# A pause in a scatter queue: a 1600-column clear against a one-element clear and a register load

## The chip, the cores and the metric
The kernel runs on one core of a Trainium2 chip. The metric is the device time of one execution in microseconds (us); the median of three runs of the kernel before is 392.05 us (391.5 to 392.49). Engines are named as the profile names them: PE is TensorE, DVE is VectorE, ACT is ScalarE, POOL is GpSimd, SP is SyncE. A "q" behind a name (POOLq, SPq) means the engine's sequencer or the transfers that it issues.

## The reference
The input is `x` of 128 x 32 x 256, that is 4096 tokens of 256 features. Two layers follow, each added to `x`.

```
# layer 0: low-rank adapters by index, then a mixture of experts
H     = x @ W.T + scaling[a] * ((x @ A[a].T) @ Bm[a].T)      # a = index of the batch row
s     = sigmoid(H @ gate_w.T)                                 # 8 experts
top 2 experts of each token; their inputs are scaled by their scores
routed = sum over k: (silu(w1 xs) * (w3 xs)) @ w2             # of the chosen expert
x     = x + routed + shared(H)
# layer 1: a conditional 32x32 mix per batch row, then Hadamard + 8-bit + ternary FFN
x     = x + FFN(mix(x))
```

What matters here is the routing of layer 0. Each token picks two of eight experts, and the kernel moves the token's row to where its expert's rows are gathered.

## The kernel before, in words
**First stage: project, route, dispatch.** The 4096 tokens are 32 tiles of 128, in 8 groups (`g`) of four. For each group, `adapt` and `project` make the rows `hc` (PE, lines 246 to 262; ACT copies them out of PSUM), and `route` finds the two experts of each token and the row that each pair gets in a DRAM buffer `xs`, which has one region per expert. The rows' numbers are in the tile `dest` (DVE, lines 271 to 334). Then `route` dispatches: for each of the group's four tiles, and for each of its two choices, one indirect transfer from POOL (line 341) scatters the tile's 128 rows of 272 columns to `xs`. That makes 64 transfers. The first group is routed in two halves, so there are nine parts (`p`).

After every second tile, that is after every four transfers, and in all groups but the last two, POOL executes a pause (line 354): a memset of a tile `pause`, which nothing reads. There are 12. The code keeps a pause in program order, and `tc.issue_after(paused[-1].ins)` queues the transfers that follow behind the last pause. Outside of that, a scheduler places the instructions of each engine. POOL's first-stage queue is: some memsets, four transfers, pause, four transfers, pause, and so on, with one gather for the second layer (`wc`, line 463) after the fourth pause, and 16 transfers without a pause at the end.

Meanwhile PE goes on to the shared expert (`shared`, lines 128 to 172) of six of the eight groups, and DVE makes the ternary weights (lines 358 to 394) and a table of tiles of rows (`slot_table`). `pad` writes zeros behind each region, from SP.

**Second stage: the experts.** `fetch` (line 528, SP) reads tiles of 128 rows of `xs` into `xin`. As the rows that it reads can come from any transfer of the dispatch, it waits for all 64. Then `turn_rows` transposes them (line 536), `gate_up` and `down` multiply by the expert's weights (lines 562 and 588), and POOL scatters the results to `yt` (line 595; these transfers have a bound `NY - 1` given as a constant). This runs in 36 steps of two tiles each, and the remaining two groups of the shared expert follow it.

**Third stage.** `combine` reads `yt` back, and the second layer runs in 16 steps of two tiles (lines 640 to 797).

Of the kernel before, what the change touches and what calls it, by code (L numbers as in the profile page):

```python
# [7 lines left out]
F32 = mybir.dt.float32  # L8
F16 = mybir.dt.float16
BF16 = mybir.dt.bfloat16  # L10
I32 = mybir.dt.int32
# [4 lines left out]
P = 128  # L16
# [6 lines left out]
E = 8  # L23
# [7 lines left out]
REG = 2 * B * T  # L31
# [20 lines left out]
def tile_kernel(  # L52
# [15 lines left out]
    nc = tc.nc  # L68
# [5 lines left out]
    small = ctx.enter_context(tc.tile_pool(name="small", bufs=3))  # L74
# [3 lines left out]
    def bank(tag, name, shape=(P, 512), dtype=F32):  # L78
        return psum.tile(list(shape), dtype, tag=tag, name=name)
# [33 lines left out]
    with tc.tile_pool(name="moe", bufs=1) as moe, tc.tile_pool(name="work1", bufs=2) as work1:  # L113
# [61 lines left out]
        with tc.tile_pool(name="stage", bufs=1) as stage:  # L175
# [28 lines left out]
            nc.sync.dma_start(ud, updown)  # L204

            zeros = stage.tile([P, ROW], F32, name="zeros")
            pause = stage.tile([P, 1600], F32, name="pause")
            cnt = stage.tile([P, E], F32, name="cnt")
            nc.gpsimd.memset(zeros, 0.0)
            nc.gpsimd.memset(cum[:, 0], 0.0)  # L210
# [53 lines left out]
            def route(p, g, tiles):  # L264

                n0, m = tiles.start, len(tiles)
                part = slice(n0, n0 + m)
                lg = hc[g][:, part, D:PROW]
                s = small.tile([P, m, E], F32, tag="s", name=f"s{p}")

                nc.vector.tensor_scalar(s, lg, -88.0, None, ALU.max)
                nc.scalar.activation(s, s, AF.Exp, scale=-1.0)
                nc.vector.tensor_scalar(s, s, 1.0, None, ALU.add)
                nc.vector.reciprocal(s, s)

                sj = s.unsqueeze(2).to_broadcast([P, m, E, E])
                se = s.unsqueeze(3).to_broadcast([P, m, E, E])
                gt = small.tile([P, m, E, E], F32, tag="gt", name=f"gt{p}")
                eq = small.tile([P, m, E, E], F32, tag="eq", name=f"eq{p}")
                nc.vector.tensor_tensor(gt, sj, se, ALU.is_gt)  # L280
                nc.vector.tensor_tensor(eq, sj, se, ALU.is_equal)
                eqf = eq.rearrange("p n e j -> p n (e j)")
                nc.vector.tensor_tensor(
                    eqf,
                    eqf,
                    tri.rearrange("p e j -> p (e j)").unsqueeze(1).to_broadcast([P, m, E * E]),
                    ALU.mult,
                )
                nc.vector.tensor_tensor(gt, gt, eq, ALU.add)
                rank = small.tile([P, m, E], F32, tag="rank", name=f"rank{p}")  # L290
                nc.vector.tensor_reduce(rank, gt, AX.X, ALU.add)
                chosen = small.tile([P, m, E], BF16, tag="ch", name=f"chosen{p}")
                nc.vector.tensor_scalar(chosen, rank, 2.0, None, ALU.is_lt)  # L293

                nc.vector.scalar_tensor_tensor(lg, rank, 2.0, s, ALU.is_lt, ALU.mult)

                to = small.tile([P, m, E], F32, tag="to", name=f"to{p}")
                t2 = pj[:, C_T2 + g * GT + n0 : C_T2 + g * GT + n0 + m]
                nc.vector.tensor_tensor(
                    to, rank, t2.unsqueeze(2).to_broadcast([P, m, E]), ALU.add  # L300
                )
                nc.vector.scalar_tensor_tensor(
                    hc[g][:, part, PROW:], rank, 2.0, to, ALU.is_lt, ALU.mult
                )


                before = small.tile([P, m, E], BF16, tag="before", name=f"before{p}")
                nc.vector.tensor_copy(before[:, 0], cum[:, p])  # L308
                for n in range(1, m):
                    nc.vector.tensor_tensor(  # L310
                        before[:, n], before[:, n - 1], chosen[:, n - 1], ALU.add
                    )
                nc.vector.tensor_tensor(
                    cum[:, p + 1], before[:, m - 1], chosen[:, m - 1], ALU.add
                )
                pp = bank("x", f"pp{p}", (P, m, E))
                nc.tensor.matmul(pp, upper, chosen, start=True, stop=False)
                nc.tensor.matmul(pp, onb, before, start=False, stop=True)
                row = small.tile([P, m, E], F32, tag="row", name=f"row{p}")
                nc.vector.tensor_tensor(  # L320
                    row,
                    pp,
                    pj[:, C_EREG : C_EREG + E].unsqueeze(1).to_broadcast([P, m, E]),
                    ALU.add,
                )
                pick = small.tile([P, 2, m, E], F32, tag="pick", name=f"pick{p}")
                for i in range(2):
                    nc.vector.scalar_tensor_tensor(
                        pick[:, i], rank, float(i), row, ALU.is_equal, ALU.mult
                    )  # L330
                df = small.tile([P, 2, m], F32, tag="df", name=f"df{p}")
                dest = small.tile([P, 2, m], I32, tag="dest", name=f"dest{p}", bufs=NG + 1)
                nc.vector.tensor_reduce(df, pick, AX.X, ALU.add)
                nc.vector.tensor_copy(dest, df)

                for n in range(m):
                    with ExitStack() as stack:
                        if paused:
                            stack.enter_context(tc.issue_after(paused[-1].ins))
                        for i in range(2):  # L340
                            ins = nc.gpsimd.indirect_dma_start(  # L341
                                out=xs,
                                out_offset=bass.IndirectOffsetOnAxis(
                                    ap=dest[:, i, n : n + 1], axis=0
                                ),
                                in_=hc[g][:, n0 + n],
                                in_offset=None,
                            ).ins
                            tc.declare_no_dep(ins, group="xs", reason="every pair has its own row")
                            tc.add_to_no_dep_group("xs", ins)  # L350
                    if n % 2 and g < NG - 2:


                        paused.append(tc.keep_in_program_order(nc.gpsimd.memset(pause, 0.0)))

            paused = []

            def ternary_weights():
                rs = stage.tile([P, 2], F32, name="rs")
# [121 lines left out]
            for g in range(1, NG):  # L481
                xa = adapt(g)
                if g == 1:
                    route(0, *parts[0])
                for n in range(GT):
                    if n == GT - 1:
                        route(g, *parts[g])
                    project(g, n, xa)
                if g == 2:
                    mixes()  # L490
            for g in range(NG):
                xg.append(cpool.tile([P, GT, D], F32, tag="x", name=f"x{g}", bufs=NG))
                nc.sync.dma_start(xg[g], xt[g])
            route(NG, *parts[NG])
            tc.keep_in_program_order(nc.vector.tensor_copy(idh, ident))
            slot_table()
# [424 lines left out]
```

## Time and profile before

| what | us |
|---|---|
| median of three runs | 392.05 |
| the profiled execution, its own time | 394.07 |
| its span, first to last instruction | 392.3 |
| PE busy | 349.2 (89%) |
| DVE busy | 248.4 (63%) |
| POOL busy | 244.0 (62%) |
| POOL, 64 dispatch transfers, line 341 | 63.5 |
| POOL, 12 pauses, line 354 | 17.4 |

The profiled execution ran 2.0 us longer than the median, and 1.8 us of its time lie outside of its span. [...] Idle time of an engine is put down to what released it; "issue" is time in which the profile shows no other wait.

### The profile page before, as it was taken

The page shows a single profiled execution, that of the slowest core. Times are in us where ns is not written, and L with a number is a line of the kernel's source. Part 1 is how long each engine was busy: PE and PEld are TensorE (multiplying, and loading weights), DVE is VectorE, ACT ScalarE, POOL GpSimd, SP SyncE. Part 2 cuts the span into 40 slices and gives each one's busy share as a digit, 9 for nine tenths or more (in the row PEclk, how much of TensorE's full clock was granted, in tenths as well). Part 3 has the DMA queues.
Part 4 walks back from the last instruction along what each step waited for, and adds up shares of the span by engine and source line. Part 5 has one row for each costly group of instructions (what it writes and reads, how often), then busy time and mean ns, then how long its engine had stood idle before and what let it go on. Part 6 is the DMA issues. An engine that isn't in the chain of part 4 may idle for free.

```text
span 392.3 us, 6604 instructions
## 1 busy us (share of the span) xinstructions
PE 349.2 (89%) x2057; PEld 275.6 (70%) x2057; DVE 248.4 (63%) x764; ACT 161.1 (41%) x329; POOL 244.0 (62%) x271
## 2 busy tenths in 40 slices
PE   4998999779990799999999999997799999999873
PEld 3675666546560588888787888855689898899762
DVE  1367986999740456465555555435778878877742
ACT  1112222222110144444344344331668787778742
POOL 4058888888874035555555365548899797855520
PEclk9999999999997599999999999999999999999986
DMA  7996458543233725555444442226523352101111
GB/s 267 420 410 232 150 181 249 181 160 128 91 115 105 222 88 156 167 158 157 148 155 149 141 136 74 83 63 232 179 94 107 103 168 82 48 34 57 53 55 53
DMA packets 37906, 57.38 MB, mean 146 GB/s; under 512 B 8941, under 2 KB 27631, under 8 KB 37488
## 3 DMA queue, kind: packets, MB, share of 16 engines
q1 hardware_dynamic: 30912, 39.06, 31.0%
q0 software_dynamic: 6672, 17.84, 12.4%
q8 instruction: 17, 0.28, 0.3%
q14 instruction: 17, 0.14, 0.1%
q10 hardware_dynamic: 288, 0.07, 0.1%
HBM read 33.81 MB, written 24.18 MB: 148 GB/s over the span
## 4 chain that ended last, share of the span: by engine, by line
PE 54%; DVE 17%; issue 9%; POOL 7%; DMA 6%; ACT 5%; SPq 1%; DVEq 0%; POOLq 0%; ACTq 0%
PE pg L562 14%; PE pr L752 7%; PE po L588 6%; PE ph L260 4%; POOL yt L595 3%; PE pf L668 3%; PE py L648 3%; PE pt_s L536 3%; DMA xs<-hc,dest 2%; PE ph L261 2%; PE pu L722 2%; PE pa L246 2%; DMA xT<-in_xT 2%; DVE chosen L293 2%; PE phd L579 1%
## 5 line engine op out<-in xcount | busy, mean ns | idle before, releaser
L595 POOL DMA_INDIRECT yt<-y,to x72 | 70.0, 973 | 68.1 <-DVE cm L545 23.7
L341 POOL DMA_INDIRECT xs<-hc,dest x64 | 63.5, 992 | 36.3 <-DVE before L308 18.6
L562 PE MATMUL pg<-wall,xTs 128*128 x288 | 78.7, 399 | 2.8 <-DVE cm L545 2.0
L562 PEld LDWEIGHTS pg<-wall,xTs 128*128 128x128 f32 x288 | 50.8, 195 | 14.8 <-DVE hid L571 4.6
L571 DVE SCALAR_TENSOR_TENSOR hid<-pg,c,sil 128x128 f32<-128x128 f32 x72 | 25.1, 348 | 44.3 <-ACT sil L570 42.5
L570 ACT ACTIVATE sil<-pg,c 128x128 f32<-128x128 f32 x72 | 26.4, 367 | 60.2 <-PE pg L562 60.0
L640 POOL TENSOR_TENSOR x<-x,y 128x512 f32<-128x512 f32 x32 | 40.5, 1268 | 6.3 <-DMA y<-yt 5.0
L588 PE MATMUL po<-wall,hidT 128*128 x144 | 37.7, 381 | 0.0
L752 PE MATMUL pr<-cst,b 128*128 128x128 f32 x256 | 35.8, 288 | 1.0 <-POOL b L741 0.5
L262 ACT COPY hc<-ph 128x264 f32<-128x264 f32 x32 | 12.1, 378 | 57.2 <-PE ph L261 51.4
L260 PE MATMUL ph<-pj,xT 128*128 128x264 f32 x128 | 35.2, 399 | 0.0
L536 PE MATMUL pt_s<-cst,xin 128*128 128x128 f32 x144 | 26.2, 286 | 9.1 <-DMA xin<-xs 9.1
L752 PEld LDWEIGHTS pr<-cst,b 128*128 128x128 f32 x256 | 32.0, 198 | 1.6 <-POOL b L741 0.9
L260 PEld LDWEIGHTS ph<-pj,xT 128*128 128x128 f32 x128 | 24.3, 194 | 8.1 <-issue 3.5
L143 PE MATMUL pgs<-hT,ws 128*128 128x512 f32 x64 | 29.1, 596 | 0.8 <-DVE hT L86 0.8
L536 PEld LDWEIGHTS pt_s<-cst,xin 128*128 128x128 f32 x144 | 19.1, 147 | 14.5 <-DMA xin<-xs 10.5
L588 PEld LDWEIGHTS po<-wall,hidT 128*128 128x128 f32 x144 | 24.5, 190 | 2.2 <-ACT hidT L88 0.3
L766 ACT ACTIVATE q<-pr,half,sc 128x512 f16<-128x512 f32 x32 | 23.3, 787 | 5.3 <-DVE sc L763 5.3
L261 PE MATMUL ph<-pj,xa 128*128 128x264 f32 x64 | 20.3, 399 | 3.5 <-DVE xa L248 3.3
L740 POOL TENSOR_TENSOR b<-c 128x512 f32<-128x512 f32 x16 | 20.3, 1267 | 4.9 <-DVE m L759 4.5
L730 ACT ACTIVATE rl<-pu 128x512 f32<-128x512 f32 x32 | 17.9, 607 | 9.9 <-PE pu L722 9.9
L668 PE MATMUL pf<-cst,yT 128*128 128x128 f32 x128 | 18.9, 285 | 3.4 <-DVE yT L660 2.0
(138 smaller groups left out, 680.7 us busy)
## 6 DMA issues: line engine op xcount, KB each, us to landing
xin<-xs SPq DMA_DIRECT2D x72, 136.0 KB, 2.4
y<-yt SPq DMA_DIRECT2D x16, 512.0 KB, 3.7
xT<-in_xT SPq DMA_DIRECT2D x8, 512.0 KB, 8.9
x<-in_x SPq DMA_DIRECT2D x8, 512.0 KB, 5.3
out<-o SPq DMA_DIRECT2D x16, 256.0 KB, 2.1
wall<-in_experts SPq DMA_DIRECT2D x2, 1536.0 KB, 12.8
yt<-y,to POOLq DMA_INDIRECT x72, 3.1
xs<-zeros SPq DMA_DIRECT2D x8, 136.0 KB, 2.0
```

The source lines that it names most:

```text
L143: nc.tensor.matmul(pg, ws13[:, k, i], hT[:, k], start=(k == 0), stop=(k == 1))
L260: nc.tensor.matmul(ph, xT[g][:, k, cols], WT[:, k], start=(k == 0), stop=False)
L261: nc.tensor.matmul(ph, xa[:, cols], BT, start=False, stop=True)
L341: ins = nc.gpsimd.indirect_dma_start(out=xs, out_offset=bass.IndirectOffsetOnAxis(ap=dest[:, i, n : n + 1], axis=0), in_=hc[g][:, n0 + n], ...
L536: nc.tensor.transpose(pt[:, i, k], xin[:, i, k * P : (k + 1) * P], ident)
L562: nc.tensor.matmul(pg[:, i].rearrange("p a f -> p (a f)"), xT[:, i, k], wall[:, bass.ds(w + k * D, D)], start=(k == 0), stop=(k == 1),)
L570: nc.scalar.activation(sil[:, i], pg[:, i, 0], AF.Silu, scale=ci)
L588: nc.tensor.matmul(po[:, i], hT[:, i], wall[:, bass.ds(w + 2 * D, D)], start=True, stop=True)
L595: ins = nc.gpsimd.indirect_dma_start(out=yt, out_offset=bass.IndirectOffsetOnAxis(ap=to[:, i : i + 1], axis=0), in_=y[:, i], in_offset=Non ...
L640: nc.gpsimd.tensor_tensor(v, v, y2[:, :, r], ALU.add)
L668: nc.tensor.matmul(pf[:, i, k * P : (k + 1) * P], yT[:, k, i * P : (i + 1) * P], hads, start=True, stop=True,)
L752: nc.tensor.matmul(pr[:, f * P : (f + 1) * P], b[:, f, i * P : (i + 1) * P], had, start=True, stop=True,)
```

## The change
The tile `pause` and its memset go. In place of it, POOL clears (here: sets) one 32-bit integer in a one-element tile `most` to `E * REG - 1`, the last row of `xs`, and loads it into a register of POOL. The register is the bound that the next dispatch transfers compare their row numbers with; before the first pause, the bound is the same number as a constant. So every dispatch transfer gets a bound, and as no row number lies above it, the same rows are written. The 12 pauses stand at the same places of POOL's queue. The instructions of the other four engines stand in the same order as before.

```
-            pause = stage.tile([P, 1600], F32, name="pause")
...
                                 in_offset=None,
+                                bounds_check=bound[0],
+                                oob_is_err=False,
                             ).ins
...
                     if n % 2 and g < NG - 2:
-                        paused.append(tc.keep_in_program_order(nc.gpsimd.memset(pause, 0.0)))
-
-            paused = []
+                        most = small.tile([1, 1], I32, tag="most", name=f"most{g}_{n0 + n}")
+                        tc.keep_in_program_order(nc.gpsimd.memset(most, E * REG - 1))
+                        r = nc.gpsimd.alloc_register(f"most{g}_{n0 + n}")
+                        paused.append(tc.keep_in_program_order(nc.gpsimd.reg_load(r, most)))
+                        bound[0] = r
+
+            paused, bound = [], [E * REG - 1]
```

The pool `small` keeps three buffers of a tag, so a `most` is written again three pauses later, when its load is over. The load waits for the memset of its own element.

## The prediction

> **What bounds the kernel now.** I began with the chain of waits, since the share of busy time (PE 89%) is a mean over stages. Around the change the chain runs through POOL and its transfers, and then into the first fetch:
>
> ```profile
> 119.61 0.96 POOL xs L341
> 120.58 0.30 issue
> 120.88 0.96 POOL xs L341
> 121.84 0.30 issue
> 122.14 2.42 DMA xs<-hc,dest
> ```
>
> The last dispatch transfer starts at 122.14 us and lands 2.42 us later, at 124.56; SP's first fetch goes out at 124.67. The waits say what hangs on that:
>
> ```profile
> SPq L528 <- DMA xs<-hc,dest: 28.7, 1, 28.7
> PE pt_s L536 <- DMA xin<-xs: 9.1, 2, 8.9
> ```
>
> SP's fetch queue stood 28.7 us, and PE, whose shared expert ended at 118.0, stood 8.9 us until 126.9. So the expert stage starts when the dispatch ends, not when PE is free. What sets the dispatch's end? POOL's timeline:
>
> ```profile
> 78.64 0.96 POOL L341 DMA_INDIRECT xs<-hc,dest  x1 [0.30 <-issue]
> 79.91 0.96 POOL L341 DMA_INDIRECT xs<-hc,dest  x1 [0.31 <-issue]
> 80.87 1.45 POOL L354 MEMSET pause<- 128x1600 f32 x1
> 82.48 0.97 POOL L341 DMA_INDIRECT xs<-hc,dest  x1 [0.17 <-DVE to L299]
> ```
>
> POOL never waits for work between 23.47 and 123.1. A transfer costs 0.96 + 0.30 = 1.26, and a pause puts 82.48 - 80.87 = 1.61 between two transfers instead of 0.30. Nor is it held by routing: `dest` of the part whose transfers start at 50.46 was ready at 44.5, the next at 51.0 for 63.38, the last at 84.8 for 113.29. The lead grows from 6 to 28 us. **POOL's own queue is the bound of this stage, and its pauses are on the path.**
>
> [...]
>
> ```profile
> 79.72 0.42 DVE L291 TENSOR_REDUCE rank<-gt 128x32 f32<-128x256 f32 x1
> 80.18 2.18 DVE L293 TENSOR_SCALAR chosen<-rank 128x32 bf16<-128x32 f32 x1
> 82.39 0.16 DVE L310 TENSOR_TENSOR before<-before,chosen 128x8 bf16<-128x8 bf16 x1
> ```
>
> A 0.18 us instruction (its time at 63.55) ended only with the pause, at 82.36. [...] So I count POOL's time per transfer and add one landing at the end. [...] No POOL load is in this trace, but others are:
>
> ```profile
> L513 PEldq TENSOR_LOAD <-tab x5: 714/1236/1297, 129.0 to 239.9; - x5
> L448 SPq TENSOR_LOAD <-ends x1: 767/767/767, 84.0 to 84.0; - x1
> ```
>
> The table's loads bring 16 registers, its last one 8, and L448 8. [...]
>
> **The change, part by part.**
> *Removed:* 12 memsets of 1.45 us, on POOL's path with their neighbourhood of 1.61 each.
> *Added, per pause:* (a) a one-element memset. The one-column memsets at the span's start took 99 to 121 ns: 0.12. (b) From its end to the load: DVE finished `tab` at 94.44 and SP's load of it began at 94.5, so 0.07. (c) The load: a straight line through 8 registers (0.74) and 16 (1.24) gives 0.30 for one; [...] 8 registers took 0.77. I take **0.60** as an estimate, with ends 0.30 and 0.77. (d) From the load's end to the next transfer's start: on SP 0.13 to its next instruction (84.77 to 84.9), and on POOL a transfer starts 0.27 to 0.29 after the tile that it awaits (`y` done at 142.05, transfer at 142.32): 0.40. Sum 0.12 + 0.07 + 0.60 + 0.40 = **1.19 for 1.61, a gain of 0.42**; with the ends of the load 0.72 and 0.25. Twelve pauses: **5.0** (8.6 and 3.0).
>
> The wait is real and cannot be hidden by POOL running ahead: without a load its sequencer does run ahead (the first `yt` bound is set at 114.5, when seven `xs` transfers had still to start), but the load waits for a memset that stands behind four transfers on POOL, and the next transfers use the register. Queued behind it on POOL are only those transfers and, once, the gather `wc`; SP's store of it (L470) has slack, its consumer is the third stage.
> *Added, per transfer:* a bound. Bounded `yt` transfers last 0.973, unbounded `xs` ones 0.961. Their rows differ in length, so this is a guess at a price: 0.012 x 64 = **0.8** lost; ends 0 and 0.8. I take 0.8.
> *Side effect on DVE:* the pauses held seven routing instructions (34.30, 41.38, 47.68, 55.51, 67.68, 73.78, 80.18) for 1.06 to 2.0 each beyond their own time, 10.9 in all, and `dnT` at 101.0 for 1.6 more. A short memset and an idle POOL free most of this. I cost it at **nothing**: routing already leads POOL, and what PE gains by finishing the shared expert sooner it spends waiting for `xin`. If the cover went, that is if the dispatch ended over 8.9 us sooner, PE would be late next, and this side effect would push that limit further away.
> *Unpriced:* [...] the total above 0.96 is 2.0 in this profile, so I allow 1 either way.
>
> Sum: -5.0 + 0.8 = **-4.2** (ends -7.8 and -2.2). All stages after the dispatch shift as a block: they hang on `xin`, and their instructions keep their order. Against the profiled execution 394.07 - 4.2 = 389.9; it stood 2.0 above the median, so the median should be 392.05 - 4.2 = **387.8**.
>
> **The rivals.**
> *A, shorter pause, as above:* 387.8, between 384.2 and 389.9.
> *B, shorter pause and PE keeps its clock.* The windows show the clock that PE was granted (last but two column):
>
> ```profile
> 122.00:124.00 2.00, 0.00 (x0) 0.00 (x0) 0.00 (x0) 0.00 (x0) 0.96 (x1) 0.83 0.36 137
> 124.00:126.00 2.00, 0.00 (x0) 0.00 (x0) 0.00 (x0) 0.00 (x0) 0.00 (x0) 0.50 0.12 15
> 132.00:134.00 2.00, 2.00 (x7) 1.54 (x7) 0.33 (x3) 0.26 (x1) 0.00 (x0) 0.50 0.84 242
> 136.00:138.00 2.00, 2.00 (x10) 1.45 (x8) 0.42 (x2) 0.73 (x2) 0.00 (x0) 0.76 0.38 119
> ```
>
> 0.83 over two us means that it fell to half at 123.3, 5.3 us after PE's last matmul, and 0.76 that it rose at 137.0. From 131.66 on PE is busy; 5.3 us at half speed cost 2.7. If the dispatch ends 4.2 sooner and PE no sooner, PE idles 4.7, and the clock might hold: 392.05 - 4.2 - 2.7 = 385.1, at best 381.5 (7.8 + 2.7). Against it: the freed DVE lets PE finish sooner by more than 0.6, and then it idles past 5.3 again.
> *C, slower: the load is dear.* If POOL's load takes what 16 registers take elsewhere, 1.24, the pause is 0.12 + 0.07 + 1.24 + 0.40 = 1.83, 0.22 over the old one: 12 x 0.22 + 0.8 = +3.4, so 395.5. It turns when the load passes 1.61 - 0.59 - 0.8/12 = 0.95. The 8-register loads (0.71 and 0.77) speak against it; that no load on POOL is seen, [...] leaves it open.
> *D, a wash:* a load of 0.87 to 1.03 gives 391.1 to 393.0.
> That the change does nothing is excluded on POOL (the old memset is gone), though not in the time, which is D.
>
> **How the numbers follow.** 0.3% is 1.2 us, about what a measurement of this kernel can tell from no change. A 0.66 and B 0.14 are faster by more: 0.80. D is 0.07, C 0.13. The range of 80% starts at B's best, 381.5, and ends at 393.0, above D: it leaves out C, and the 1 us of POOL's stretching is within it. Most likely: 387.8.
>
> **What would show it.** In the profile after: no 1.45 us memsets; 12 loads on POOL's sequencer of about 0.6; 1.2 between the transfers around a pause; transfers of 0.97; the last one starting near 118; routing instructions without 2 us outliers; PE idle before the first transpose, with the same fall of the clock (or without, B). A gap over 1.6 around the pauses makes me wrong by C. If the last transfer starts at 118 and the time stays, then the fetch was not bound by the dispatch; if it starts sooner than the gaps explain, transfers were cheaper. A POOL that waits for `dest` would refute that routing leads.

## The result, and the profile after

The kernel with the short pause takes 390.31 us (median of 19 runs, 389.18 to 391.59), the kernel before on the same chip 393.16 (19 runs). The ratio is 0.9935, with a 95% interval of 0.9919 to 0.9951 (the ratio is that of the means; the medians alone differ by 2.85): 2.6 us faster, between 1.9 and 3.2. The forecast was 4.2. A run over 1.5% above the fastest of its kernel is left out of the figures below; that is one of six of e3. The profiled execution took 391.13 with a span of 389.4, against 394.07 and 392.3: 2.9 less in both.

POOL's timeline after, at the pause that the prediction showed of before (start, duration, engine and line, what it writes and reads, and in brackets the idle time before it):

```profile
84.62 1.08 POOL L340 DMA_INDIRECT xs<-hc,dest  x1 [0.30 <-issue]
85.69 0.09 POOL L357 MEMSET most<- 1x1 int32 x1
86.96 0.97 POOL L340 DMA_INDIRECT xs<-hc,dest  x1 [1.18 <-DVE tab L446]
```

The memset now takes 0.09, and 1.27 lie between the two transfers, where it was 1.61. The engine named in the bracket is only what ended nearest; `tab` is nothing that the transfer reads. The load is not a busy piece of POOL, but it is listed under its sequencer (minimum/median/maximum in ns, first and last start):

```profile
L359 POOLq TENSOR_LOAD <-most x12: 287/296/673, 28.7 to 99.0; - x12
```

The chain after, at the end of the dispatch, and the two waits that hang on it (total, times, longest):

```profile
119.01 0.30 issue
119.32 2.42 DMA xs<-hc,dest
...
121.86 0.37 SPq L534
```

```profile
SPq L534 <- DMA xs<-hc,dest: 33.6, 1, 33.6
```

```profile
PE pt_s L542 <- DMA xin<-xs: 14.2, 2, 14.0
```

The last transfer starts at 119.32 instead of 122.14. The first one stood at 23.62 (before 23.47), so the dispatch, from the start of its first transfer to the start of its last, takes 95.70 instead of 98.67. That is 2.97 less, and it is all of the 2.9 of the span: behind it everything moved as a block. In three terms:

| from the first transfer's start to the last one's end, us | before | after |
|---|---|---|
| the 12 gaps around pauses | 19.33 | 16.69 |
| POOL's 65 transfers (64 and `wc`) | 64.45 | 64.14 |
| the 52 other gaps, 0.30 each | 15.85 | 15.85 |

Seven of the twelve gaps are 1.22 to 1.31, five are 1.46 to 1.81; the mean is 1.39. Transfers did get longer by the bound (median 0.961 to 0.972), but in this execution they were stretched less, so their sum shrank. On DVE the long routing instructions are gone:

```profile
L292 DVE TENSOR_SCALAR chosen<-rank x9: 174/181/366, 19.0 to 74.6; 128x32 bf16<-128x32 f32 x7, 128x16 bf16<-128x16 f32 x2
```

Its maximum was 2.18 us and is 0.37; DVE's busy time fell from 248.4 to 237.5. PE's shared expert ends at 110.1 instead of 118.0, and PE then waits 14.0 instead of 8.9.

### The profile page after: what moved, and what is told of

It reads as the page before. It is cut to its first block, busy times and chain, and to the rows that moved or that the text cites. A ratio compares the mean times of both kernels' runs of the same rounds, so it can differ in the third digit from the quotient of the medians.

```text
span 389.4 us, 6628 instructions
## 1 busy us (share of the span) xinstructions
PE 347.9 (89%) x2057; PEld 275.5 (71%) x2057; DVE 237.5 (61%) x764; ACT 161.2 (41%) x329; POOL 227.8 (59%) x271
## 4 chain that ended last, share of the span: by engine, by line
PE 66%; issue 8%; POOL 7%; DMA 7%; DVE 5%; ACT 4%; SPq 1%; POOLq 0%; DVEq 0%; ACTq 0%
PE pg L568 14%; PE ph L259 7%; PE pr L758 7%; PE po L594 6%; PE ph L260 4%; PE pgs L143 4%; PE pa L245 4%; POOL yt L601 3%; PE pf L674 3%; PE py L654 3%; PE pt_s L542 3%; DMA xs<-hc,dest 3%; PE pu L728 2%; PE pos L158 2%; DMA xT<-in_xT 2%
## 5 line engine op out<-in xcount | busy, mean ns | idle before, releaser
L340 POOL DMA_INDIRECT xs<-hc,dest x64 | 63.2, 987 | 48.7 <-DVE before L307 19.9
```

The source lines that it names most:

```text
L340: ins = nc.gpsimd.indirect_dma_start(out=xs, out_offset=bass.IndirectOffsetOnAxis(ap=dest[:, i, n : n + 1], axis=0), in_=hc[g][:, n0 + n], ...
```

## The experiments

Each ratio is against runs of the kernel before on the same chip; its median there was 396.93 for the e runs, 392.52 for f, 397.24 for g, 392.77 for h and 392.98 for i. Between chips I compare the dispatch as the trace has it (98.67 before, 95.70 after).

### Repeat

**f1_changed_again**, the changed kernel unaltered, on another chip:

> The changed kernel as it is, so that it stands beside the others on one chip. Both theories: the ratio lies between 0.980 and 0.995 (0.9935 at first; a constant bound gave 0.980 on another chip, where the kernel before itself was 4 us longer). Last dispatch transfer near 119.3, expert stage from 124.

389.46, ratio 0.9926 (0.9899 to 0.9953). Its twelve gaps sum to 16.27, and the dispatch takes 95.74. So the two executions of this kernel that were profiled have 16.3 and 16.7.

### What does a pause consist of?

**e4_short_clear** is the kernel before with a one-element memset in the pause, no load and no bound. **e1_standing_element** sets the element once at the start, and each pause only loads it.

```
 e4:  -    paused.append(tc.keep_in_program_order(nc.gpsimd.memset(pause, 0.0)))
      +    paused.append(tc.keep_in_program_order(nc.gpsimd.memset(pause[0:1, 0:1], 0.0)))
 e1:  +    most = stage.tile([1, 1], I32, name="most")      # once, at the start
      +    nc.gpsimd.memset(most, E * REG - 1)
      ...
      -    most = small.tile(...)                           # in each pause
      -    tc.keep_in_program_order(nc.gpsimd.memset(most, E * REG - 1))
```

> The kernel before with one edit: each pause clears one element of the tile, at the same place of the queue, and there is no load and no bound. Theory: nothing stops the sequencer; the gap around a pause falls from 1.61 to about 0.30, the last transfer starts 12 x 1.31 = 15.7 us sooner, near 106.4, DVE's stalls of 2 us go, PE becomes the bound when its shared expert ends near 110, and the time is about 0.957 of before (375). Rival 1 (the pauses are of use: without them DVE or the routing is held up by POOL and its transfers): POOL waits for row numbers, the shared expert ends later than 112, and the time is less than 5 us below before. Rival 2 (the fetch is not bound by the last transfer): time unchanged within 1 us.

> The changed kernel with one edit: the element is set once at the start, and each pause is only the load of it into the register; the load has no memset behind the four transfers to wait for. Theory (the pause costs what it does because it stops POOL's sequencer until its engine has drained, so the work on the next transfer, 0.8 us from the load's end to the start, is no longer done ahead): the sequencer gets through the load while the transfers before it still run, the gap around a pause falls from 1.37 to about 0.30, the last dispatch transfer starts 12 x 1.07 = 12.8 us sooner, near 106.5; PE, done with the shared expert near 110, becomes the next bound, its clock stays up, and the time is about 15 us below the changed kernel, near 375. Rival (the load itself, or the register in the transfer, costs the 0.8 us): the gaps stay above 1 us, the last transfer near 118 to 119, the time within 1.5 us of the changed kernel's.

In both, the gap fell to 0.30 wherever POOL had its row numbers. POOL's timeline of e4:

```profile
27.53 0.09 POOL L354 MEMSET pause<- 1x1 f32 x1
27.84 0.96 POOL L341 DMA_INDIRECT xs<-hc,dest  x1 [0.21 <-issue]
```

So a short memset by itself is free: it fits into the 0.30 that lies between two transfers anyway. So is a load whose element was written long ago. The loads of e1 took the same 294 ns, but the sequencer made them while POOL was still at earlier transfers:

```profile
L359 POOLq TENSOR_LOAD <-most x12: 287/294/516, 25.4 to 89.7; - x12
```

The last load starts at 89.7, the last transfer at 120.12. Yet both kernels became slower: e1 410.39 (1.0334, 1.0304 to 1.0365), e4 410.75 (1.0343, 1.0311 to 1.0375), for a reason that comes further down.

**e2_constant_bound** is the changed kernel with a constant in place of the register. **e3_two_loads** adds a second load to a register that nothing reads:

```
 e2:  -    bounds_check=bound[0],
      +    bounds_check=E * REG - 1,
 e3:  +    again = nc.gpsimd.alloc_register(f"again{g}_{n0 + n}")
      +    tc.keep_in_program_order(nc.gpsimd.reg_load(again, most))
```

> The changed kernel with the memset and the load kept, but every transfer's bound is the constant; the register is loaded and not used. Theory (stopped sequencer): the gaps stay at 1.37 and the time is that of the changed kernel within 0.5 us (0.993 to 0.995 of before). Rival (a transfer with a register as its bound starts later): the gap falls by about 0.4 to 0.95, and the time by about 5 us, to 0.981 of before.

> The changed kernel with a second load of the same element into another register in each pause. Theory: a load costs its own duration (0.29 to 0.67, mean 0.39) and the restart of 0.8 is paid once, so the gap grows by 0.3 to 0.4, 12 times: 3.5 to 4.7 us more than the changed kernel, about 1.002 to 1.006 of before. Rival (the 0.8 is a shadow of every load): the gap grows by 1.1 to 1.2, 13 to 14 us more, about 1.027 of before.

These two have to be read with care. A load to a register that nothing reads did not run; only its wait for the memset remained. The trace of e2 shows it, as it has no load at all:

```profile
L359 POOLq EVENT_SEMAPHORE  x12: 17/17/17, 27.7 to 95.8; - x12
```

In e3, 12 loads ran, not 24. So e2 is a pause of memset and wait, and it shows what the wait alone costs:

```profile
33.52 0.09 POOL L357 MEMSET most<- 1x1 int32 x1
34.59 1.10 POOL L340 DMA_INDIRECT xs<-hc,dest  x1 [0.97 <-issue]
```

The gap is still 1.03 typically (the twelve sum to 12.87, the dispatch takes 93.31). e2 took 389.53, ratio 0.9804 (0.9772 to 0.9836); that is 7.8 us, more than the 5.4 of its dispatch. e3, where an empty wait of 17 ns was added, has gaps of 1.33 instead of 1.26, and 391.54 (0.9876, 0.9842 to 0.9911); that is 4.9 us for 2.6 of its dispatch. So both gained 2.3 to 2.4 us beyond their dispatch on this chip, and the surplus does not belong to the constant bound. It may be the kernel before that is hindered there; no trace of it on this chip was kept. Neither run prices a load.

Two more runs do. **i1_two_live_loads** has two loads, one for the transfers of each choice; **i2_load_read_late** keeps one load and lets only the fourth transfer behind it read the register.

```
 i1:  -    bounds_check=bound[0],
      +    bounds_check=bound[i],
      ...
      +    for i in range(2):                       # alloc_register, reg_load, bound[i] = r
 i2:  -    bounds_check=bound[0],
      +    bounds_check=bound[0] if n % 2 and i else E * REG - 1,
```

> The changed kernel with two loads of the same element in each pause, one for the transfers of each choice, so that both registers are read. Theory S (POOL's sequencer executes loads one after the other and starts the next transfer only behind them): each pause grows by a load's 0.29 us as the trace has it, from 1.26 to 1.55 typically, 12 x 0.29 = 3.5 us in all, which takes up the change's gain: last transfer some 99.2 us after the first, the time within 0.3% of the kernel before. Rival O (the loads overlap, or their time lies within the restart of about 0.9 us): 0 to 0.1 more per pause, at most 1 us in all, time as the changed kernel's.

> The changed kernel with the register as the bound of the fourth transfer behind a pause only, the other three with the constant: the load stays in the program at its place. Theory S (a load costs its place in the order): the pauses take 1.26 typically, as in the changed kernel, and the sum over the twelve stays at 16.3 to 16.7. Rival U (the transfer that reads the register waits for it): the pause falls to the 1.02 of the kernel whose load is gone, the sum to 12.9, and the fourth transfer loses nothing, since its load is long over: 3.5 us sooner than the changed kernel's last transfer.

i1: 395.79, ratio 1.0070 (1.0050 to 1.0089), slower than the kernel before. The trace has both loads, and gaps of 1.60 to 2.12 that sum to 22.00:

```profile
L360 POOLq TENSOR_LOAD <-most x24: 285/302/763, 28.4 to 105.1; - x24
```

```profile
34.92 0.09 POOL L357 MEMSET most<- 1x1 int32 x1
36.54 0.97 POOL L340 DMA_INDIRECT xs<-hc,dest  x1 [1.53 <-DVE eq L282]
```

Here the loads took 0.287 and 0.291 and the gap is 1.62, against 1.26 at the same pause of the changed kernel: the second load's 0.29, and 0.06 between the two. Over all twelve, the second load added 22.00 - 16.5 = 5.5 where 3.5 was forecast (16.5 being the mean of the changed kernel's two executions), that is 0.46 each, more than the median of a load, since some take 0.5 to 0.76. i2: 390.18 (0.9922, 0.9899 to 0.9945), gaps of 1.29 to 1.33 typically with a sum of 16.85, nearly as in the changed kernel (0.05 more each) and far from the 12.9 of the rival:

```profile
35.02 0.09 POOL L357 MEMSET most<- 1x1 int32 x1
36.36 0.97 POOL L340 DMA_INDIRECT xs<-hc,dest  x1 [1.25 <-DVE eq L280]
```

The transfer behind the pause doesn't read the register and still waits. So **a load costs its own time in the sequencer's order** (theory S), and whether the next transfer needs it makes no difference. The rivals, overlap and waiting at the use, fall.

**A pause is then: memset 0.09, 0.03 to the load, load 0.29, and 0.83 to 0.91 (0.85 in the mean) from the load's end to the next transfer.** That last term, the restart, is the largest, and e2 has about as much without a load (1.03 less the memset and its wait). It also stands in the trace of before, at the first transfer of all. POOL's sequencer waits for the first row numbers until 22.6, and its transfer starts at 23.47, some 0.9 later:

```profile
L341 POOLq EVENT_SEMAPHORE  x1: 17/17/17, 22.6 to 22.6; - x1
```

```profile
23.47 1.12 POOL L341 DMA_INDIRECT xs<-hc,dest  x1 [18.59 <-DVE before L308]
```

### What does the bound cost?

**g2_long_clear_with_bound** is the kernel before with a constant bound on the dispatch transfers.

```
      +    bounds_check=E * REG - 1,
      +    oob_is_err=False,
```

> Before with the bound of the dispatch transfers given as a constant, its 1600-column clears kept: the cost of the bound alone. The prediction's term: 64 x 0.011 to 0.012 = 0.7 to 0.8 us slower, transfers of 0.972 instead of 0.961, pauses of 1.61 as before. Rival: the bound costs nothing on the path, since the changed kernel's transfers show it by their duration only: 0.0.

398.20, ratio 1.0014 (0.9989 to 1.0039): by time it can't be told from nothing. Nor does the time hang on the dispatch here: PE's shared expert ends at 129.4, 3.4 us behind SP's first fetch at 125.9 (the reason comes below). In the trace the pauses are 1.61 as before, POOL's 65 transfers sum to 65.36 instead of 64.45, and the dispatch takes 99.57 instead of 98.67. That is near the forecast 0.7 to 0.8, and it compares two chips.

### How many pauses, and where?

**f2_early_pauses** is the changed kernel with pauses in the first two groups only (`g < 2`, four pauses), **f3_late_pauses** with the other eight (`2 <= g < NG - 2`); **f4_early_long_clears** is the kernel before with its long clears in the first two groups only.

```
           -    if n % 2 and g < NG - 2:
 f2, f4:   +    if n % 2 and g < 2:
 f3:       +    if n % 2 and 2 <= g < NG - 2:
```

> The changed kernel with pauses only in the first two groups, 4 in place of 12; from the third group on the transfers follow each other. Theory P (what went wrong without pauses is that POOL's sequencer overtakes the routing and parks at a wait for row numbers while transfers are outstanding, and PE's signals to the other engines stay away meanwhile; from the third group on the routing leads by more than the eight transfers that the sequencer runs ahead): no signal delays, the last transfer starts 8 x 1.07 = 8.6 us sooner, near 110.7, and the time is 8 to 11 us below the changed kernel (8.6, and up to 2.7 more if PE's clock stays up). Rival S (a stream of transfers without stops holds PE's signals by itself): delays of 1.5 us and more between the rank matmul and the row instruction from 50 us on, and the time at or above that of the kernel before.

> The changed kernel with pauses only from the third to the sixth group, 8 in place of 12. Theory P: the sequencer reaches the parts of the second and third group before their row numbers; PE's signals are late near 31 and 42 us, by 1.5 us each, and after that the pauses keep POOL behind, so no delay of 5 us or more follows; time within 4 us of the changed kernel, the saved 4 x 1.07 against the waits. Rival S: the first stall is as without pauses, the later part clean: the same; this run tells where the stalls lie, and f2 between the theories.

> The kernel before (1600-column clears, no bound, no load) with pauses only in the first two groups. Theory P: the last transfer starts 8 x 1.31 = 10.5 us sooner than in the kernel before, near 111.6, no signal delays beyond 2 us, time near 0.973 of before; it also tells what the load is worth where the pauses are few: f2 should lie within 2 us of it. Rival S: stalls from 50 us on, time at or above before.

As to the eight transfers by which f2's expectation has the sequencer run ahead: in the trace of before, its last wait of line 341 starts at 113.2, when eight of the 64 transfers had still to start.

f2: 382.23, ratio 0.9762 (0.9727 to 0.9797), dispatch 88.27. f3: 386.58 (0.9858, 0.9823 to 0.9892), dispatch 92.83. f4: **382.06** (0.9736, 0.9704 to 0.9767), dispatch 88.92. Eight pauses fewer brought f2 7.2 us against f1, its dispatch being 7.5 shorter; four fewer brought f3 2.9, and 2.9 in the dispatch; eight long ones fewer brought f4 10.5, and 9.8. So time follows the dispatch nearly one to one over this whole reach, on this chip. f2 and f4 have overlapping intervals: with four pauses, which kind they are no longer shows. Both beat both kernels.

PE still waits at this point. Of f4, PE's first transposes, and a stretch of the windows (busy time of PE, PEld, DVE, ACT, POOL, then the granted clock):

```profile
116.47 1.31 PE L536 MATMUL pt_s<-cst,xin 128*128 128x128 f32 x4 [4.27 <-DMA xin<-xs]
```

```profile
114.00:116.00 2.00, 0.00 (x0) 0.00 (x0) 0.00 (x0) 0.00 (x0) 0.00 (x0) 0.83 0.27 72
116.00:118.00 2.00, 1.31 (x4) 0.57 (x4) 0.55 (x3) 0.00 (x0) 0.00 (x0) 0.50 0.74 199
```

f3's expectation was wrong in one point: the late signals that it forecast without early pauses did not come.

### Why do no pauses at all make it slower?

**g1_no_pause** removes all twelve, **g3_two_long_clears** keeps the two of the first group, and **h1_one_block** puts four long clears in a row at the first pause and none after it.

```
 g1:  -    if n % 2 and g < NG - 2:
      -        paused.append(tc.keep_in_program_order(nc.gpsimd.memset(pause, 0.0)))
 g3:  -    if n % 2 and g < NG - 2:
      +    if n % 2 and g < 1:
 h1:  -    if n % 2 and g < NG - 2:
      -        paused.append(tc.keep_in_program_order(nc.gpsimd.memset(pause, 0.0)))
      +    if n % 2 and not paused:
      +        for _ in range(4):
      +            paused.append(tc.keep_in_program_order(nc.gpsimd.memset(pause, 0.0)))
```

> Before without its 12 pauses: nothing stands between the 64 transfers. Each pause put 1.31 us (1.61 - 0.30) into the dispatch, so without hindrance the last transfer starts 12 x 1.31 = 15.7 us sooner, near 106, and PE's shared expert becomes the later of the two: the time falls by 11 to 15 us, to about 380. That is the forecast of the theory that only a short memset or load between every four transfers brought PE's late signals (8 to 9 us between a matmul `pp` and DVE's `row`). The rival: what brought them is that POOL's sequencer parks at a wait for row numbers while many of its transfers are outstanding, whatever stands between; then they appear here as well, three or four of 1.5 to 9 us, and the time is near 410, some 15 above the kernel before.

> Before with its 1600-column clears in the first group alone: 2 pauses instead of 12. Against 4 pauses (382 us) two fewer take 2 x 1.31 = 2.6 us from the dispatch: last transfer near 109. PE's shared expert ended at 112.2 there and stays the same, so PE would wait only about 2 us for its first rows, and the time falls to about 379.5 if no signal comes late. Rival: with the pauses gone POOL catches up with the routing sooner, parks, and PE's signals come late by several us: over 385.

> Before with four clears of 1600 columns in a row at the first pause, and no pause after it. Two pauses of the first group (in the kernel with two long clears) did not keep PE's signals in time, four pauses in the first two groups did. If what matters is how far POOL is held behind the routing, 4 x 1.45 us at once do as well as four pauses: POOL never waits for row numbers for over 3.5 us after it, no signal is late, last transfer near 111.5, and the time is some 2.6% below the kernel before. If it matters that pauses stand between the transfers of the first two groups, late signals of 4 to 10 us come back from about 40 us on, and the time is some 4% above it.

g1: 413.42, ratio 1.0414 (1.0372 to 1.0456). g3: 413.27 (1.0416, 1.0365 to 1.0468). h1: 383.08 (0.9750, 0.9721 to 0.9779). What costs the time in e1, e4, g1 and g3 is the same: PE has done a matmul of the routing, and DVE or ACT, which wait for it, learn of it late. Of e4, PE's and DVE's timeline:

```profile
74.44 0.18 PE L318 MATMUL pp<-before,onb 128*128 128x32 bf16 x1
```

```profile
82.97 0.19 DVE L320 TENSOR_TENSOR row<-pp,pj 128x32 f32<-128x32 f32 x1 [8.79 <-remote]
```

From `pp` to `row` are 8.53 us; in the kernel before, the changed one and all f runs it is 0.22 to 0.26 in eight of the nine parts (the first takes 1.26 everywhere). In g1 five are longer (1.8, 1.6, 7.2, 8.4 and 2.7); the chain of waits books such a time to something outside of the profile's engines:

```profile
44.26 14.67 another core or an unknown queue
```

Each late signal makes the next row numbers late, so POOL waits too: g1 has four gaps of 1.8 to 5.0 that lengthen the dispatch by 15.1, nearly the 15.7 by which the twelve pauses did. And PE, which waits for the same routing, ends its shared expert at 145.2 instead of 118.0. It is PE now that is late, and not the dispatch, whose last transfer landed some 23 us before.

A pause of any kind is not what prevents this: e1 and e4 have all twelve, but of no length, and h1 has one block of length, and nothing late:

```profile
28.36 5.91 POOL L353 MEMSET pause<- 128x1600 f32 x4
34.43 0.97 POOL L341 DMA_INDIRECT xs<-hc,dest  x1 [0.16 <-issue]
```

From 34.4 on, no wait of POOL's sequencer for row numbers is over 43 ns in h1. The longest such waits are 3.1 us in the kernel before and in f3, without a late signal, and 10 to 11 us in e1, e4, g1 and g3. So it looks as if signals come late when POOL has caught up with the routing. **That is not shown**, for three reasons.

First, the chip. All traces with late signals come from the two chips of the e and g runs, on which the kernel before takes 396.9 and 397.2; the traces of before and after, and all of f, h and i, have none, and on their chips before takes 392.5 to 393.2. No kernel without pauses, or with pauses of no length, was run on those. So g3 and g1 stand on another chip than f4, f3 and h1, to which they are compared. Up to 48 us, f3 and g1 have the same POOL queue but for the constant bound; at the third part `row` comes 1.8 us after `pp` in g1 and 0.24 in f3.

Second, signals also came late with POOL far behind the routing. In g2 the last row numbers are ready at 85.7, the last transfer starts at 123.4, and from 45 on POOL's sequencer never waits over 43 ns for row numbers. Still, PE's `pgs`, a matmul of the shared expert, is done at 120.34, DVE goes on with it 3.4 us later, and PE waits in turn (timeline of g2):

```profile
116.74 3.60 PE L143 MATMUL pgs<-hT,ws 128*128 128x512 f32 x8
123.76 0.69 DVE L150 TENSOR_TENSOR hids<-pgs,sils 128x512 f32<-128x512 f32 x1 [5.05 <-remote]
124.50 2.07 PE L158 MATMUL pos<-ws,hids 128*128 128x256 f32 x4 [3.30 <-issue]
```

In e2 the same pair is 4.4 us apart (107.92 to 112.32).

Third, a late signal itself makes POOL wait: in g3 the `pp` at 49.30 was late by 10.75, and POOL's sequencer began to wait at 50.7.

What is shown is that on one chip the pauses' length matters: among the e runs, e3 (pauses of 1.33) has no late signal, e2 (1.03) some of up to 4.4, e1 and e4 (0.30) several of up to 9.3; among the g runs, g2 (twelve long clears) has some of up to 3.4, g1 and g3 several of up to 8.4 and 10.8. And in eleven of the twelve cases in which `row` started over 2.6 us after `pp`, it started 2.6 to 3.1 us after the end of POOL's last transfer. What holds the signal back stays open; h1 on the chip of the g runs, or g1 on that of h1, would tell the chip from the pauses.

## Why the prediction was right or wrong

**What limits the stage: right.** POOL's queue set the end of the dispatch, and its pauses lay on the path. The f and i runs show it both ways: the dispatch of f4 is 9.8 shorter and the time 10.5, that of i1 3.6 longer and the time 2.8.

**Removed, 12 x 1.61: right**, 19.33 by the trace.

**The step that failed: the sum of the new pause, in its term (d), "0.40".** By term, with what was measured: (a) memset 0.12, measured 0.09; (b) to the load 0.07, measured 0.03; (c) load 0.60, measured 0.29 at the median and 0.39 in the mean; (d) from the load's end to the next transfer 0.40, measured 0.85. The errors of (c) and (d) nearly cancelled, so that the typical pause, 1.26, is close to the forecast 1.19. But the gain is the difference to 1.61, and there 0.07 more is a sixth of it; the five longer pauses (a slow load, or a memset that took 0.58) add 0.13 to the mean. 1.61 - 1.39 = 0.22 remains of 0.42, and 12 x 0.22 = 2.6 of 5.0. The forecast time, 387.8, lies 2.5 below the measured 390.31 for a second reason: it was counted from 392.05, the median of three runs, and the 19 runs have 393.16. That is 1.1 of the 2.5, and the sum the rest.

Why 0.40 was wrong: both rows that it came from were of another kind. SP's 0.13 led to an instruction, not to an indirect transfer of POOL. And the `yt` transfer that starts 0.27 after its tile follows no wait of POOL's sequencer that has to end first, as I now read it (its bound was set at 114.5, 28 us ahead; argued, not tried). The right row stood in the same trace: the first dispatch transfer, 0.87 behind the end of the sequencer's wait. I had used it only as the start of the dispatch.

For (c), 0.60 was my estimate, which no row of the trace showed, set above the 0.30 that the line through the trace's own loads gave. The changed kernel's loads took 0.287 at the least and 0.296 at the median: the line was right.

**The bound's 0.8: right** as far as the trace can tell (0.7 by the medians, 0.9 in g2).

**Side effects.** DVE was freed as said, and it brought nothing, as said: PE ended 7.9 sooner and waited longer. That the limit at which PE becomes late would move is shown by f4, whose dispatch ends 10.4 sooner with PE still 4.3 early. The stretched transfers (the longest 1.285 before and 1.302 after), left at 1 either way, brought the 1 in this execution: the sum above the median was 63.5 - 64 x 0.961 = 2.0 and is 63.2 - 64 x 0.972 = 1.0. So the whole sum is -2.6 + 0.7 - 1.0 = -2.9, the change of the span.

**Rival B, wrong on its threshold.** It took 5.3 us of idle PE as what the clock needs to fall. After, PE stopped at 110.1, and this row of the windows says that the clock fell at about 113.5, after 3.4:

```profile
112.00:114.00 2.00, 0.00 (x0) 0.00 (x0) 0.00 (x0) 0.00 (x0) 1.60 (x2) 0.88 0.32 118
```

In f4, where PE was idle for just 4.3, it fell as well, after some 3.1 (0.83 in the row shown above). By the means of those rows, the fall came some 5.3, 3.4 and 3.1 us after PE's last matmul (before, after, f4): the delay is not the same each time, and 5.3 from one execution was no limit.

**Rival C, right in its mechanism.** It put the turn to slower at a load of 0.95, or a pause longer than 1.61 less the bound's share. One load is far from it; two loads (i1, mean pause 1.83) are past it, and the time is 0.7% above the kernel before.

**Not foreseen:** PE's late signals. The changed kernel's two traces have none, but both are from chips on which no trace has one; on the e chip, e3 with pauses of nearly the same length has none either.

## What to carry to other kernels

When a change replaces one wait by another, its gain is a small difference of two large terms, so price the new one from a row in which the same engine stops and starts again for the same kind of work, not from the fastest hand-over in the trace. What was dear in this pause was neither the clear (0.09 us) nor the load (0.29), but the restart (0.85) after the sequencer had stopped for something queued behind its own transfers; an element written early made the load free (e1, gaps of 0.30). And before making a pause cheaper, ask how many are needed: eight fewer brought 7 to 10 us, the cheaper kind 2.6, and none at all cost 16, this last on another chip. When runs are spread over chips, set each conclusion beside the chips that it rests on.

## What the runs showed of the hardware that I had not expected

- Where POOL's sequencer had stopped, 0.83 to 0.92 us passed from the end of its wait or load to the start of the next indirect transfer (before, after, e2); where it had run ahead, 0.30 lay between two transfers, and a one-element memset of 0.09 (e4) or a ready load of 0.29 (e1) fitted into that.
- One-register loads on POOL took 0.29 to 0.30 us at the median (after, e1, f1, i1, i2), with single ones up to 0.78 (f3), and they added up one behind another (i1: 0.46 more per pause for the second load).
- A load to a register that nothing reads left only its wait (e2: no load and 12 waits of 17 ns; e3: 12 loads, not 24): count the loads in the trace before reading such an experiment.
- On two of the chips, PE's finished matmuls reached DVE and ACT up to 10.8 us late (0.24 otherwise), most of all where the pauses were few or had no length. With four long clears at the start, 5.9 us, none was late, but on another chip.
